# Strip sums on VectorE, expert weights loaded further ahead, a new order of products at the seams, and zero rows for dt

## The chip, the cores and the metric

The kernel runs on one core of one Trainium2 chip. The metric is the device time of one execution in microseconds, given as the median of three runs. Engines are named as in the profile: PE is TensorE (its matmuls; PEld its weight loads), DVE is VectorE, ACT is ScalarE, POOL is GpSimd, and SP is SyncE, which here only issues DMAs. ScalarE's queue issues DMAs too.

## The reference, cut to what matters

The input x has three images of 256 channels of 48 x 48 pixels. Four layers follow, each added to its input after a group norm of 32 groups:

```
x = x + layer0(gn(x))   # 1x1 convs, 2 blocks of attention + MLP, concat, 1x1 conv, norm, silu
x = x + layer1(gn(x))   # routing = sigmoid(mean(x) @ R); w = sum_e routing[e] * weight[e]; 3x3 conv
x = x + layer2(gn(x))   # 3x3 conv with one fixed weight and a bias
x = x + layer3(gn(x))   # Mamba block: in_proj, conv1d, selective scan, gate, out_proj
```

Layer 1 has eight experts, and each image has its own mixed 3x3 kernel of 256 x 256 channels. In layer 3, `dt = softplus(dt_raw @ dt_proj_w + dt_proj_b)` with a dt_raw of 16 columns, for 512 inner channels, and the state has 16 entries for each of them.

## The kernel before, in words

Channels lie on partitions: 256 channels are two tiles of 128 (`CT = 2`). An image of 2304 pixels is walked in six strips of 384 (`NCH = 6`, `CH = 384`). The images are taken in the order 2, 1, 0 (`ORDER`). Everything is float32.

Layer 0 ends, for each image, with an MLP stage and then a concatenation stage, six strips each. In `hidden` (L515 on) TensorE makes two products (L520) and ScalarE applies Gelu (L525, tile f); in `add_back` TensorE multiplies f (L531) and VectorE adds the result to `cur` (L535). In `concatenated` (L1031 on) TensorE runs eight matmuls a strip (L1035) over three loaded rows (`yc`) and `cur`; ScalarE applies Silu (L1040) into the resident image `xs[b]`; GpSimd adds the strip of the kernel's input `xc` (L1045), which is the residual. `yc` and `xc` are loaded by DMAs that stand in ScalarE's queue (L1021 and L1026). `take_stats` (L1047 on) then has VectorE take the statistics of a strip (L1049) for the next group norm; it is called one strip later.

Beside these stages runs the preparation of layer 1 for image 2. `mixed` is a generator: each step loads one piece of an expert's kernel (128 x 768, 384 KB, SP's queue, L251; eight experts times six pieces) and adds it with the expert's routing weight into `u`. The first expert's six pieces are copied and scaled on ScalarE (L294), the others are added on VectorE (L296). After 48 pieces, two steps of `kernel_transform` (L258 to L263, six operations each on VectorE) turn the three columns of the kernel into six: this is a Winograd form of the 3x3 convolution along one direction, in which 0 and 2 of the six stay the mixed columns themselves. `aside(n)` (above the loop at L1064 on) takes n steps of the mixing after each strip, and so sets the order by hand: two, or in image 0's hidden stage two and three in turn, and three in the concatenation stages; from the third strip of image 0 it takes all the rest. The pieces rotate through six buffers (`wst`). The order in which instructions are written is the order on each engine (`keep_order`).

At strip 3 of image 0 the pools for the first padded and transformed image are allocated and `input_transform` (L308 on) is called: ScalarE writes the normalised image with borders (`xpad`, L331), and VectorE makes the six transformed inputs `vt` of one half image in twelve operations (L345 to L356).

Layers 1 and 2 are six units (two layers by three images), each of two halves. `output` (L1641 on) makes, for a half h and an output tile m, six products of six matmuls each (`products`, L1634): products 1 and 3, then 4 and 5 (of each pair one is copied by ScalarE into `cb`, L1650, and VectorE makes their sum and difference), then 0 and 2; VectorE adds all of them into the image. Beside unit 0 the kernel of image 1 is mixed, beside unit 1 that of image 0. There, one of the six pieces of each expert is mixed on TensorE instead (L282).

In layer 3 the strips of all three images are walked as one chain, 18 strips, with VectorE's scan (L1949) as its heart. `project_dt` (L1323 on) multiplies dt_raw by the projection; its operand `k.dbc[: DTR + 1, :]` has 16 rows and a row of ones for the bias, out of a tile of 96 rows that also holds B and C of the scan. The weight tile `dtsb` has 17 rows, loaded from `dtw` (L1153), which the host code lays out. `take_sum` (L1362) multiplies the finished dt by u on VectorE; L1355 are the matmuls that it waits for, L1971 those of the output projection of the states.

Of the kernel before, what the change touches and what calls it, by code (L numbers as in the profile page):

```python
# [9 lines left out]
F32 = mybir.dt.float32  # L10
I32 = mybir.dt.int32
AF = mybir.ActivationFunctionType
ALU = mybir.AluOpType
# [71 lines left out]
def net(  # L85
# [160 lines left out]
        nc.vector.tensor_scalar(t[:, 1, :], sh, 1.0 / 6.0, None, ALU.mult)  # L246
        return t[:, 0, :], t[:, 1, :]

    def part_of_kernel(src, ct, dx):
        t = wst.tile([P, 3 * 256], F32, name="wconv")  # L250
        nc.sync.dma_start(t, src[ct * P : (ct + 1) * P, dx * 768 : (dx + 1) * 768])  # L251
        return t.rearrange("p (y o) -> p y o", y=3)

# [8 lines left out]
        nc.vector.tensor_tensor(u[:, 3, :, ct, :], t, g1, ALU.subtract)  # L262
        nc.vector.tensor_tensor(g1, t, g1, ALU.add)  # L263

    def mixed(b, pool, shared=False):

        u = weights[b] = pool.tile([P, 6, 3, CT, 256], F32, name="u")  # L270
        for e in range(EXPERTS):
            for ct in range(CT):
                for dx in range(3):
                    wt = part_of_kernel(we[e], ct, dx)
                    re = route[b][:, e : e + 1]
                    dst = u[:, dx, :, ct, :]
                    if shared and ct == CT - 1 and dx == 2:
                        flat = wt.rearrange("p y o -> p (y o)")
                        each = tmp.tile([P, P], F32, name="each")
                        nc.scalar.activation(each, ident, AF.Copy, scale=re)  # L280
                        for j in range(2):
                            nc.tensor.matmul(  # L282
                                bank[j], each, flat[:, j * 384 : (j + 1) * 384],
                                start=e == 0, stop=e == EXPERTS - 1,
                            )
                        if e == EXPERTS - 1:
                            for y, o, n in ((0, 0, 256), (1, 0, 128), (1, 128, 128), (2, 0, 256)):
                                at = y * 256 + o
                                j = at // 384
                                nc.scalar.copy(  # L290
                                    dst[:, y, o : o + n], bank[j][:, at - 384 * j : at - 384 * j + n]
                                )
                    elif e == 0:
                        nc.scalar.activation(dst, wt, AF.Copy, scale=re)  # L294
                    else:
                        nc.vector.scalar_tensor_tensor(dst, wt, re, dst, ALU.mult, ALU.add)  # L296
                    yield
        for ct in range(CT):
            kernel_transform(u, ct)
            yield  # L300
# [15 lines left out]
    def input_transform(b, h, sc, sh):  # L316

        rows = HR + 2
        size = rows * PW
        t = pad.tile([P, 4, CT * size + 2], F32, name="xpad")  # L320

        nc.gpsimd.memset(t[:, :, 0 : CT * size + 1 : PW], 0.0)  # L322
        at = (0 if h == 0 else HR + 1) * PW
        for ct in range(CT):
            nc.gpsimd.memset(t[:, :, ct * size + at : ct * size + at + PW], 0.0)
        lo = 1 if h == 0 else 0
        first = h * HR - 1 + lo
        for ct in range(CT):
            src = xs[b][:, ct, :].rearrange("p (j r c) -> p j r c", j=4, c=TW)
            dst = t[:, :, ct * size : (ct + 1) * size].rearrange("p j (r c) -> p j r c", c=PW)  # L330
            nc.scalar.activation(  # L331
                dst[:, :, lo : lo + HR + 1, 1:], src[:, :, first : first + HR + 1, :],
                AF.Identity, bias=sh[:, ct : ct + 1], scale=sc[:, ct : ct + 1],
            )

        def column(j, at):
            return t[:, j, at : at + CT * size].rearrange("p (r c) -> p r c", c=PW)[:, :, :TW]

        d = [column(j, at) for j, at in ((3, 0), (0, 1), (1, 1), (2, 1), (3, 1), (0, 2))]
        vt = vp.tile([P, 6, CT, (HR + 2) * TW], F32, name="vt")  # L340
        o = [vt[:, i].rearrange("p t (r c) -> p (t r) c", c=TW) for i in range(6)]
        c = pad.tile([P, CT * rows, TW], F32, name="wc")
        e = pad.tile([P, CT * rows, TW], F32, name="we")
        tt, stt = nc.vector.tensor_tensor, nc.vector.scalar_tensor_tensor
        stt(c, d[2], -4.0, d[4], ALU.mult, ALU.add)  # L345
        stt(e, d[1], -4.0, d[3], ALU.mult, ALU.add)
        tt(o[1], c, e, ALU.add)
        tt(o[3], c, e, ALU.subtract)
        tt(c, d[4], d[2], ALU.subtract)
        tt(e, d[3], d[1], ALU.subtract)  # L350
        stt(o[4], e, 2.0, c, ALU.mult, ALU.add)
        stt(o[5], e, -2.0, c, ALU.mult, ALU.add)
        tt(o[0], d[0], d[2], ALU.subtract)
        stt(o[0], o[0], 4.0, c, ALU.mult, ALU.add)
        tt(o[2], d[5], d[3], ALU.subtract)
        stt(o[2], e, -4.0, o[2], ALU.mult, ALU.add)  # L356
        return vt

    def routing(b, psum, tag, stats):
# [23 lines left out]
    with ExitStack() as l0:  # L383
# [627 lines left out]
        upools = {0: late_pool("up0")}  # L1011
        xpools[1] = late_pool("x1")
        xpools[0] = late_pool("x0", stack=last_pools)
        for b in ORDER:
            xs[b] = xpools[b].tile([P, CT, N], F32, name=f"x{b}")

# [7 lines left out]
        def tokens_of(b, c):  # L1024
# [3 lines left out]
            )  # L1028
            return xc

        def concatenated(b, c, yc, xc):  # L1031
            pz = pair()
            for m in range(2):
                for kt in range(4):
                    nc.tensor.matmul(  # L1035
                        pz[:, m, :CH], w("cv2", kt * 256 + m * P, P),
                        yc[:, kt, :] if kt < 3 else chunk(cur[b], c), start=kt == 0, stop=kt == 3,
                    )
            for m in range(2):
                nc.scalar.activation(  # L1040
                    chunk(xs[b][:, m, :], c), pz[:, m, :CH], AF.Silu,
                    bias=b2sh[:, m : m + 1], scale=b2sc[:, m : m + 1],
                )
            both = xs[b][:, :, c * CH : (c + 1) * CH]
            nc.gpsimd.tensor_tensor(both, both, xc, ALU.add)  # L1045

        def take_stats(b, c, stats):  # L1047
            for m in range(2):
                nc.vector.bn_stats(stats[m][:, c, :], chunk(xs[b][:, m, :], c))  # L1049

# [3 lines left out]
        ahead = [(rows_of(*chunks[z]), tokens_of(*chunks[z])) for z in range(3)]  # L1054
        rows_ahead, tokens_ahead = ([pair[j] for pair in ahead] for j in range(2))
        small_steps = [mlp_weights(i, 0)]
        mixing = mixed(2, upools[0])

        def aside(n):

# [9 lines left out]
        for n, b in enumerate(ORDER):  # L1070
            held = None
            for c in range(NCH):
                f = hidden(b, c)
                if held is not None:
                    add_back(i, *held)
                held = b, c, f
                aside(3 if n == 2 and c % 2 else 2)
            add_back(i, *held)
            stats = [
                small.tile([P, NCH, 6], F32, name=f"xst{m}", bufs=2) for m in range(CT)  # L1080
# [1 line left out]
            for c in range(NCH):  # L1082
                concatenated(b, c, rows_ahead.pop(0), tokens_ahead.pop(0))

                z = n * NCH + c + 2
                if 3 <= z < len(chunks):
                    tokens_ahead.append(tokens_of(*chunks[z]))
                if z + 1 < len(chunks):
                    rows_ahead.append(rows_of(*chunks[z + 1]))
                if c:  # L1090
                    take_stats(b, c - 1, stats)
                if b == 0 and c == 3:
                    vp = late_pool("vp", 2, last_pools)
                    pad = late_pool("pad", stack=last_pools)
                    first_v = input_transform(2, 0, *norms[2])
                aside(3 if n < 2 or c < 2 else 99)
            take_stats(b, NCH - 1, stats)
            if b:
                curpools[b].close()
# [34 lines left out]
    def w3_rooms():  # L1134
# [4 lines left out]
            block, ("w3sb", P, (NW3,)), ("winx", P, (CT, DI * P)), ("taps", P, (DI, DCONV, P)), ("convc", P, (DI * DCONV,)),  # L1139
            ("amat", P, (DI * DS,)), ("rep", P, (4, 32)), ("less", P, (2, P)), ("zero", P, (8,)),  # L1140
            ("xn0", P, (CT, XH)), ("xn1", P, (CT, XH)), ("xi", P, (3, XH)),
            ("dtsb", DTR + 1, (DI * P,)),
        ))
        rooms["xn"] = [w3v["xn0"], w3v["xn1"]]
        pieces = [wst.tile([P, 3 * 256], F32, name="wconv") for _ in range(6)]
# [177 lines left out]
    def project_dt(k, m0):  # L1323
        for j in range(2):
            m = m0 + j
            nc.tensor.matmul(
                bank[j], w3v["dtsb"][:, m * P : (m + 1) * P], k.dbc[: DTR + 1, :],
                start=True, stop=True,
            )

# [293 lines left out]
    with ExitStack() as l1:  # L1624
# [17 lines left out]
        def output(b, h, m, u, vt, bias):  # L1642

            xj = xs[b][:, m, :].rearrange("p (j n) -> p j n", j=4)[:, :, h * HN : (h + 1) * HN]
            tt, stt = nc.vector.tensor_tensor, nc.vector.scalar_tensor_tensor
            sums = []
            for i, j in ((1, 3), (4, 5)):
                pa, pb = products(u, vt, m, i), products(u, vt, m, j)
                cb = tmp.tile([P, HN], F32, name="cb")
                nc.scalar.copy(cb, pb)  # L1650
# [2 lines left out]
                sub = tmp.tile([P, HN], F32, name=f"sub{i}")  # L1653
                tt(sub, pa, cb, ALU.subtract)
                sums += [add, sub]
            p, q, r, s = sums
            for k, (minus, more, f) in enumerate(((p, r, 1.0), (q, s, 2.0), (p, r, 4.0), (q, s, 8.0))):
                if bias is None:
                    tt(xj[:, k], xj[:, k], minus, ALU.subtract)
                else:  # L1660
                    stt(xj[:, k], xj[:, k], bias[:, m : m + 1], minus, ALU.add, ALU.subtract)
                stt(xj[:, k], more, f, xj[:, k], ALU.mult, ALU.add)
            for i, k, f in ((0, 0, 1.5), (2, 3, 6.0)):
                stt(xj[:, k], products(u, vt, m, i), f, xj[:, k], ALU.mult, ALU.add)


        units = [(layer, b) for layer in range(2) for b in ORDER]
# [506 lines left out]
def _layout(i):  # L2174
# [39 lines left out]
        "w3": np.concatenate([w3[k] for k, _ in W3_WIDTHS], 1),  # L2214
        "w3x": l3["in_proj_w"][: DI * P].T,
        "convw": l3["conv_w"].reshape(DI, P, DCONV).transpose(1, 0, 2).reshape(P, -1),
        "dtw": np.concatenate([l3["dt_proj_w"].T, l3["dt_proj_b"][None]]),
    }


# [17 lines left out]
```

## Time and profile before

| | us |
|---|---|
| median of three runs | 3303.44 (3302.32 to 3303.94) |
| profiled execution | 3306.9 |
| its span, first to last instruction | 3305.1 |
| busy in it: PE, DVE, ACT, POOL | 3140.9, 2867.9, 2393.1, 1338.7 |
| mean granted TensorE clock | 0.983 of full |

The profile is one execution, taken on the slowest core, here the only one. It gives times of groups of instructions (a line of the kernel, an engine, an operation with its tiles), and names for idle time the event that ended it. A wait for several events is put down to the one that came last by the record. In rows of groups, "x42 | 44.8, 1119 | 0.0" is the number of instructions, their busy time in us, the mean of one in ns, and the idle time of the engine just before them. In rows of waits, the three numbers are the sum, the number of times, and the longest, in us. Layer 0's attention lasts until about 1322 us, the last MLP and concatenation stages until 1491, the convolutions until about 1997, and layer 3 to the end.

### The profile page before, as it was taken

The page shows a single profiled execution, that of the slowest core. Times are in us where ns is not written, and L with a number is a line of the kernel's source. Part 1 is how long each engine was busy: PE and PEld are TensorE (multiplying, and loading weights), DVE is VectorE, ACT ScalarE, POOL GpSimd, SP SyncE. Part 2 cuts the span into 40 slices and gives each one's busy share as a digit, 9 for nine tenths or more (in the row PEclk, how much of TensorE's full clock was granted, in tenths as well). Part 3 has the DMA queues.
Part 4 walks back from the last instruction along what each step waited for, and adds up shares of the span by engine and source line. Part 5 has one row for each costly group of instructions (what it writes and reads, how often), then busy time and mean ns, then how long its engine had stood idle before and what let it go on. Part 6 is the DMA issues. An engine that isn't in the chain of part 4 may idle for free.

```text
span 3305.1 us, 54212 instructions
## 1 busy us (share of the span) xinstructions
PE 3140.9 (95%) x20918; PEld 1557.1 (47%) x20918; DVE 2867.9 (87%) x3225; ACT 2393.1 (72%) x3675; POOL 1338.7 (41%) x457
## 2 busy tenths in 40 slices
PE   7999999999999999998999998999999999999996
PEld 4334343363343434556677774444444444444442
DVE  3799989967988999389985449999999999999998
ACT  2688888848888888332223458888888888888885
POOL 0000000000000000120000008999999999999998
PEclk9999999999999999999999999999999999999998
DMA  4000000010000000484621025555555555555552
GB/s 168 32 8 10 7 10 6 8 48 5 8 7 8 8 7 9 153 313 165 222 80 42 34 75 132 139 129 128 136 130 142 140 138 130 130 134 137 141 132 69
DMA packets 182657, 290.98 MB, mean 88 GB/s; under 512 B 34850, under 2 KB 148962, under 8 KB 180467
## 3 DMA queue, kind: packets, MB, share of 16 engines
q1 hardware_dynamic: 169426, 268.53, 30.1%
q10 hardware_dynamic: 12960, 18.88, 1.7%
q8 instruction: 166, 2.72, 0.3%
q14 instruction: 105, 0.85, 0.1%
HBM read 236.24 MB, written 50.64 MB: 87 GB/s over the span
## 4 chain that ended last, share of the span: by engine, by line
PE 55%; DVE 28%; ACT 8%; issue 5%; DMA 2%; POOL 1%; SPq 0%; DVEq 0%; ACTq 0%; POOLq 0%
DVE hs L1949 19%; PE ps_s L640 16%; PE acc L653 15%; PE ps_c L1634 8%; DVE hs L1896 3%; ACT ps_da L1941 2%; PE ps_s L1035 2%; PE ps_y L464 2%; DVE u L296 2%; PE ps_m L667 2%; PE ps_m L713 1%; PE acc L531 1%; PE ps_g L1229 1%; PE ps_s L520 1%; DMA wconv<-in_we 1%
## 5 line engine op out<-in xcount | busy, mean ns | idle before, releaser
L644 ACT ACTIVATE pt<-ps_s 128x1024 f32<-128x1024 f32 x972 | 942.4, 1022 | 154.7 <-PE ps_s L640 142.2
L1949 DVE TENSOR_TENSOR_SCAN hs<-ps_da,hs 128x385 f32<-128x385 f32 x1152 | 1002.6, 936 | 5.6 <-ACT ps_da L1941 4.5
L859 DVE TENSOR_TENSOR part<-part,pt 128x2048 f32<-128x2048 f32 x396 | 906.7, 2290 | 41.2 <-ACT pt L644 18.4
L1941 ACT ACTIVATE ps_da<-dtr,u 128x384 f32<-128x384 f32 x1136 | 642.0, 580 | 116.2 <-DVE hs L1949 105.5
L164 POOL TENSOR_TENSOR rstd<-ve,mhalf 128x2 f32<-128x2 f32 (+1 forms) x25 | 16.0, 642 | 1440.6 <-DVE ve L162 1440.6
L640 PE MATMUL ps_s<-q,kt 32*128 32x512 f32 (+1 forms) x4320 | 576.4, 592 | 0.1
L653 PE MATMUL acc<-pt,vt 128*32 128x512 f32 (+1 forms) x4320 | 520.9, 561 | 0.2
L1634 PE MATMUL ps_c<-vt,u 128*128 128x288 f32 x1728 | 431.9, 410 | 17.6 <-DVE u L263 9.0
L1957 POOL TENSOR_TENSOR hc<-hs,x 128x3072 f32<-128x3072 f32 x72 | 405.3, 5629 | 11.2 <-DVE hs L1949 6.7
L1957 POOL TENSOR_TENSOR hc<-hs,bc 128x3072 f32<-128x3072 f32 x71 | 400.2, 5636 | 9.8 <-POOL hs L1915 3.9
L1634 PEld LDWEIGHTS ps_c<-vt,u 128*128 128x128 f32 x1728 | 330.0, 192 | 114.3 <-DVE u L263 9.7
L640 PEld LDWEIGHTS ps_s<-q,kt 32*128 32x128 f32 x4320 | 195.2, 183 | 199.1 <-issue 120.2
L653 PEld LDWEIGHTS acc<-pt,vt 128*32 128x32 f32 x4320 | 94.4, 108 | 353.4 <-issue 326.7
L1971 PE MATMUL ps_y<-hc,u 128*32 128x384 f32 x2304 | 226.9, 514 | 2.9 <-POOL hc L1957 2.9
L1915 POOL TENSOR_TENSOR hs<-dtur,bc 128x1536 f32<-128x1536 f32 x72 | 209.8, 2913 | 0.0
L1280 PE MATMUL ps_g<-u 128*128 128x384 f32 x576 | 193.6, 488 | 11.6 <-ACT u L1276 11.6
L1915 POOL TENSOR_TENSOR hs<-dtur,x 128x1536 f32<-128x1536 f32 x70 | 203.5, 2907 | 0.0
L1280 PEld LDWEIGHTS ps_g<-u 128*128 128x128 f32 x576 | 107.5, 189 | 94.2 <-ACT u L1276 22.5
L1971 PEld LDWEIGHTS ps_y<-hc,u 128*32 128x32 f32 x2304 | 62.2, 112 | 144.0 <-issue 128.7
L1650 ACT COPY cb<-ps_c 128x288 f32<-128x288 f32 x48 | 19.2, 399 | 150.7 <-PE ps_c L1634 141.5
L322 POOL MEMSET xpad<- 128x212 f32 x12 | 5.7, 475 | 291.6 <-ACT xpad L1685 221.5
L1399 PE MATMUL ps_g<-u 128*128 128x384 f32 x288 | 106.6, 503 | 13.1 <-ACT sz L1407 7.7
(295 smaller groups left out, 4169.8 us busy)
## 6 DMA issues: line engine op xcount, KB each, us to landing
wconv<-in_we SPq DMA_DIRECT2D x144, 384.0 KB, 4.6
dtr<-dtd SPq DMA_DIRECT2D x284, 192.0 KB, 3.7
dtur<-dtud SPq DMA_DIRECT2D x284, 96.0 KB, 4.2
wconv<-xd SPq DMA_DIRECT2D x36, 384.0 KB, 4.0
x<-bcd SPq DMA_DIRECT2D x72, 192.0 KB, 4.9
dtd<-x SPq DMA_DIRECT2D x36, 384.0 KB, 3.0
bc<-bcd SPq DMA_DIRECT2D x72, 192.0 KB, 5.0
dtuq<-dtud SPq DMA_DIRECT2D x284, 48.0 KB, 2.0
```

What stands on the lines that cost most here:

```text
L640: nc.tensor.matmul(s[:, j, cols], kt[r, mt * P : (mt + 1) * P], q[r, :n], start=True, stop=True,)
L644: nc.scalar.activation(p[:, h0 : h0 + 2, :], s, AF.Exp)
L653: nc.tensor.matmul(acc[h * HD : (h + 1) * HD, :n], vt[:, mt, g * P + h * HD : g * P + (h + 1) * HD], p[:, h, cols], start=mt == 0, stop=mt ...
L859: ): nc.vector.tensor_tensor(part, first, p, ALU.add)
L1280: nc.tensor.matmul(bank[m % 2], w3v["taps"][:, m, tap, :], w3v["xi"][:, m % 3, tap : tap + CH], start=tap == 0, stop=tap == DCONV - 1,)
L1399: nc.tensor.matmul(bank[j], w("in", ct * 512 + m * P, P), k.xn[:, ct, DCONV - 1 :], start=ct == 0, stop=ct == CT - 1,)
L1634: nc.tensor.matmul(pc[:, :HN], u[:, i, dy, ct, m * P : (m + 1) * P], vt[:, i, ct, dy * TW : dy * TW + HN], start=ct == 0 and dy == 0, stop ...
L1915: nc.gpsimd.tensor_tensor(states(s)[:, :, 2:4, 1:], chunks[at].rows[m][1].unsqueeze(1).broadcast_to([P, 2, 2, CH]), b_rows(s, 0, 2), ALU.mult,
L1941: nc.scalar.activation(slots[n % 3][:, 1 : CH + 1], chunks[at].rows[m][0][:, q, :], AF.Exp, scale=amat[:, col : col + 1],)
L1949: nc.vector.tensor_tensor_scan(b, slots[(8 * s + part) % 3][:, : CH + 1], b, 0.0, ALU.mult, ALU.add)
L1957: nc.gpsimd.tensor_tensor(hc, tiles[s][:, :, :, 1:], cb.broadcast_to([P, 2, 4, CH]), ALU.mult)
L1971: nc.tensor.matmul(k.y_ps[32 * q : 32 * q + 32, :CH], fold, hc[:, g, q, :], start=False, stop=g == 1 and q in ends,)
```

## The change

In layer 0's last stages the strip sum goes from GpSimd in `concatenated` to VectorE in `take_stats`, directly ahead of the statistics and one strip later than before; so the buffer of `xc` is released by VectorE. `take_stats` is called ahead of the next loads. Pieces 6 to 13 of image 2's kernel get eight buffers of their own (`wst2`), on top of the six. Each hidden strip takes three steps of mixing. The rest of the mixing with the kernel transforms comes at strip 1 of image 0 instead of strip 2, and `input_transform` at strip 2 instead of 3, where the eight buffers are given back.

In layers 1 and 2, for the first half of a unit the transform writes its outputs in the order 0, 2, 4, 5, 1, 3 instead of 1, 3, 4, 5, 0, 2, and the first output tile takes its products in the order 0, 2, then 4 and 5, then 1 and 3. The second half and the other tile keep the old order.

In layer 3 the weights of `project_dt` get 79 rows of zeros, so that they have 96 rows, and the matmul runs over the whole tile `k.dbc`.

```diff
-    def part_of_kernel(src, ct, dx):
-        t = wst.tile([P, 3 * 256], F32, name="wconv")
+    def part_of_kernel(src, ct, dx, pool=None):
+        t = (pool or wst).tile([P, 3 * 256], F32, name="wconv")
...
-    def mixed(b, pool, shared=False):
+    def mixed(b, pool, shared=False, second=None):
...
-                    wt = part_of_kernel(we[e], ct, dx)
+                    at = (e * CT + ct) * 3 + dx
+                    wt = part_of_kernel(we[e], ct, dx, second if 6 <= at < 14 else None)
...
+        def odd():
+            stt(c, d[2], -4.0, d[4], ALU.mult, ALU.add)
+            stt(e, d[1], -4.0, d[3], ALU.mult, ALU.add)
+            tt(o[1], c, e, ALU.add)
+            tt(o[3], c, e, ALU.subtract)
+
+        def outer():
+            tt(o[0], d[0], d[2], ALU.subtract)
+            stt(o[0], o[0], 4.0, c, ALU.mult, ALU.add)
+            tt(o[2], d[5], d[3], ALU.subtract)
+            stt(o[2], e, -4.0, o[2], ALU.mult, ALU.add)
+
...
-        stt(c, d[2], -4.0, d[4], ALU.mult, ALU.add)
-        stt(e, d[1], -4.0, d[3], ALU.mult, ALU.add)
-        tt(o[1], c, e, ALU.add)
-        tt(o[3], c, e, ALU.subtract)
+        if h:
+            odd()
         tt(c, d[4], d[2], ALU.subtract)
         tt(e, d[3], d[1], ALU.subtract)
+        if not h:
+            outer()
         stt(o[4], e, 2.0, c, ALU.mult, ALU.add)
         stt(o[5], e, -2.0, c, ALU.mult, ALU.add)
-        tt(o[0], d[0], d[2], ALU.subtract)
-        stt(o[0], o[0], 4.0, c, ALU.mult, ALU.add)
-        tt(o[2], d[5], d[3], ALU.subtract)
-        stt(o[2], e, -4.0, o[2], ALU.mult, ALU.add)
+        if h:
+            outer()
+        else:
+            odd()
...
+        more_pools = ExitStack()
+        wst2 = late_pool("wst2", 8, more_pools)
...
+            added[b, c] = xc
+
+        def take_stats(b, c, stats):
             both = xs[b][:, :, c * CH : (c + 1) * CH]
-            nc.gpsimd.tensor_tensor(both, both, xc, ALU.add)
-
-        def take_stats(b, c, stats):
+            nc.vector.tensor_tensor(both, both, added.pop((b, c)), ALU.add)
...
-        mixing = mixed(2, upools[0])
+        mixing = mixed(2, upools[0], second=wst2)
...
-                aside(3 if n == 2 and c % 2 else 2)
+                aside(3)
...
+                if c:
+                    take_stats(b, c - 1, stats)
                 if 3 <= z < len(chunks):
                     tokens_ahead.append(tokens_of(*chunks[z]))
                 if z + 1 < len(chunks):
                     rows_ahead.append(rows_of(*chunks[z + 1]))
-                if c:
-                    take_stats(b, c - 1, stats)
-                if b == 0 and c == 3:
+                if b == 0 and c == 2:
+                    more_pools.close()
                     vp = late_pool("vp", 2, last_pools)
                     pad = late_pool("pad", stack=last_pools)
                     first_v = input_transform(2, 0, *norms[2])
-                aside(3 if n < 2 or c < 2 else 99)
+                aside(3 if n < 2 or c < 1 else 99)
...
-            ("dtsb", DTR + 1, (DI * P,)),
+            ("dtsb", 96, (DI * P,)),
...
-                bank[j], w3v["dtsb"][:, m * P : (m + 1) * P], k.dbc[: DTR + 1, :],
+                bank[j], w3v["dtsb"][:, m * P : (m + 1) * P], k.dbc,
...
+            def ends():
+                for i, k, f in ((0, 0, 1.5), (2, 3, 6.0)):
+                    stt(xj[:, k], products(u, vt, m, i), f, xj[:, k], ALU.mult, ALU.add)
+
+            first = h == 0 and m == 0
+            if first:
+                ends()
             sums = []
-            for i, j in ((1, 3), (4, 5)):
+            for i, j in ((4, 5), (1, 3)) if first else ((1, 3), (4, 5)):
...
-            p, q, r, s = sums
+            p, q, r, s = sums[2:] + sums[:2] if first else sums
...
-            for i, k, f in ((0, 0, 1.5), (2, 3, 6.0)):
-                stt(xj[:, k], products(u, vt, m, i), f, xj[:, k], ALU.mult, ALU.add)
+            if not first:
+                ends()
...
-        "dtw": np.concatenate([l3["dt_proj_w"].T, l3["dt_proj_b"][None]]),
+        "dtw": np.concatenate(
+            [l3["dt_proj_w"].T, l3["dt_proj_b"][None], np.zeros((95 - DTR, DI * P), np.float32)]
+        ),
```

More of the change, by code (lines that the diff above doesn't have):

```diff
@@ L1029, in tokens_of @@
             return xc
+        added = {}
         def concatenated(b, c, yc, xc):
```

## The prediction

> **What bounds the kernel now.** I read the rows of busy tenths first (which stage leaves which engine free), then the waits of TensorE over the one stage that the change touches, then its windows, and then the groups of VectorE and GpSimd there. Below, "pieces" are the 384 KB expert weights, "mixing" is L296 on VectorE (one step a piece), and times are microseconds of the profiled execution.
>
> ```profile
> PE   7999999999999999998999998999999999999996
> DVE  3799989967988999389985449999999999999998
> ```
>
> A slice is 82.6 us. Attention (to about 1322) and the scan of layer 3 (slices 24 on, from about 1997) hardly change; the scan is bound by VectorE, so time gained before it is kept whole. The change works between 1322 and 1700, slices 16 to 20.
>
> ```profile
> PE ps_c L1634 <- ACT u L294: 7.4, 1, 7.4
> PE acc L531 <- ACT f L525: 4.1, 1, 4.1
> PE ps_r L376 <- DVE pbc L373: 0.3, 1, 0.3
> ...
> PE ps_c L1634 <- DVE u L263: 7.2, 1, 7.2
> PE ps_g L282 <- DMA wconv<-in_we: 1.3, 2, 0.8
> ...
> PE ps_c L1634 <- DVE u L263: 1.8, 1, 1.8
> PE ps_c L1634 <- DVE u L262: 1.1, 1, 1.1
> ```
>
> The waits of TensorE over 1400 to 1500, 1500 to 1620 and 1620 to 1720: total, times, longest. There are four places: 4.1 before the last MLP's concatenation (at 1437.9 to 1441.9), 7.4 at the first convolution product ("seam A", 1490.7 to 1498.1), 7.2 between the first two images' convolutions ("seam B", 1584.2 to 1591.8), 1.8 and 1.1 at the next ("seam C", 1675.4). From 1700 to 2000 TensorE is busy 298.11 of 300: that stretch starts earlier by whatever the seams give.
>
> ```profile
> 1480.00:1500.00 20.00, 12.58 (x38) 7.45 (x37) 19.69 (x19) 10.50 (x13) 7.02 (x6) 0.89 0.46 157
> ...
> 1580.00:1600.00 20.00, 12.70 (x38) 8.38 (x37) 19.94 (x26) 12.76 (x18) 0.69 (x3) 0.74 0.67 230
> ```
>
> Windows: length, busy time of PE, PEld, DVE, ACT, POOL, granted clock, DMA share, GB/s. VectorE is full in both seams (19.69 and 19.94 of 20), TensorE is not. So the release that ends the 7.4 is named ACT, but the late engine is VectorE: the first product started at 1498.09, right after the transform L347 that it reads ended (1497.83). And the clock falls after each gap (0.89, 0.74): the first two products of unit 0 took 8.5 and of unit 1 9.1, against 6.14 (12 matmuls of 0.41 twice over, less overlap) later. A gap therefore costs 2 to 3 more than its length.
>
> ```profile
> L296 DVE SCALAR_TENSOR_TENSOR u<-wconv,route,u 128x768 f32<-128x768 f32 x42 | 44.8, 1119 | 0.0
> L1049 DVE BATCH_NORM_STATS2 xst<-x 128x6 f32<-128x384 f32 x30 | 15.3, 549 | 40.1 <-POOL x L1045 40.1
> ...
> L260 DVE SCALAR_TENSOR_TENSOR u<-u,wconv 128x768 f32<-128x768 f32 x2 | 3.5, 1755 | 0.0
> L262 DVE TENSOR_TENSOR u<-wconv,u 128x768 f32<-128x768 f32 x2 | 3.4, 1712 | 0.1
> ...
> L1045 POOL TENSOR_TENSOR x<-x,xc 128x768 f32<-128x768 f32 x18 | 36.9, 2052 | 93.8 <-ACT x L1040 78.7 <-DMA wconv<-in_we 15.2
> ```
>
> Groups between 1324 and 1498. The strip sum takes GpSimd 2052 ns, and whatever VectorE does beside it stretches: L260 1755 in the mean against 951 for its sister L258, which met no sum.
>
> **The change part by part.**
>
> *Strip sums to VectorE.* Added: 18 times a two-input 128x768 operation; the nearest row is L261, the same form, 958 ns: 18 x 0.96 = 17.3. Taken away: the stretching. Of the kernel transforms the eight instructions of L259, L260, L262 and L263 took 3.4 + 3.5 + 3.4 + 3.5 = 13.8 against 8 x 0.96 = 7.7: 6.2 back (unrounded). Of L296: 42 x (1.119 - 1.011, its median without sums) = 4.5 back. Net +6.6 over the stage, but VectorE idled 40.1 there, waiting for these same sums, so only the last strips count: in seam A four sums (strips 2 to 5) = +3.8 against -6.2. [...] by the row (2.45 instead of 0.96 beside a sum) it is 2.4 earlier. I take the row.
>
> *Eight more pieces, mixing a strip sooner.* No DMA more in number: the same 144 pieces, eight of them issued on SP's queue earlier, at a time when it is idle. Before the last concatenation 45 mixing steps are done instead of 39, so 6 x 0.95 = 5.7 of VectorE leave the way to seam A. ScalarE gets three first-expert pieces of 0.9 ahead of its activation f where it had two; TensorE's L531 there waits about 1.5 longer. The 4.1 wait goes in good part, for it was ScalarE held by its queue (a table load at 1440.0 that a piece let go, with the DMAs at 369 GB/s, share 1.02): -3.5. But in the last hidden stage six strips have 3 mixings instead of 2 or 3, 18 instead of 15, 2.9 more on VectorE ahead of pbc (L373), which TensorE's L376 waits for; I get +3.6 there in place of the 0.3 shown. Sum -3.5 + 3.6, about 0 (bounds -3.5 and +3.6): the last concatenation starts at 1459.2 as before and ends at 1490.7.
>
> *Order in seam A.* VectorE afterwards: sum 0 at 1467, twelve kernel transforms 1468.9 to 1480.1 (12 x 0.93), sum 1 at 1481, the input transform (12 of 0.8). ScalarE: the load of the next xc stands in its queue and now waits for VectorE's sum 1, then xpad (2.67) to 1484.7; input transform 1484.7 to 1494, its fourth output ready at 1489.4; then ScalarE's Silu of strip 3 (1.23), the second xpad to 1495.2 (it waits until the transform has read the first), Silu of strips 4 and 5 to 1498.3. The first product waits for those Silus' bank: 1498.5. What VectorE gains, ScalarE's queue gives back: +0.4. Bounds: with no hold the products could follow strip 5's Silu at 1492, -6; with every held step taken in full +3. I take the walk.
>
> *Unit 0.* VectorE still owes three sums, the statistics and the routing chain of the last image, among the first products: L186, L195 and L376 stand in TensorE's order there. I put +2.1 on the sixth product (bounds 0 and +4). Unit 0 ends at 1584.2 + 0.4 + 2.1 = 1586.7.
>
> *Seam B.* VectorE's mixing for the next image ends sooner by 6.2 + 5.7 - 3.8 = 8.1: at about 1575.5 for 1583.6. The new order puts products 0 and 2 first, which use mixed weights that no transform touches, so TensorE starts at once and has 6.1 of work until products 4 and 5, whose transform is then ready (about 1585). The wait of 7.6 (1584.2 to 1591.8) goes, with 2.5 of the slow clock after it.
>
> *Seam C.* The same order gives 6.1 of slack and VectorE is 8.1 ahead for a TensorE 7.6 ahead: of 1.8 + 1.1, I take 2.4 back (bounds 0 and 2.9).
>
> *Zero rows for dt.* L1326 contracts 96 rows instead of 17. Its duration should not move (481 at 17 rows; L1355 at 128 rows 486). Its weights' one load grows from 34 KB to 196 KB; it runs on SP's queue during layer 2's convolutions, where the DMA share is 0.16 and TensorE waits for nothing of it: 0. What can move is the clock: in the scan the clock is halved in six windows of 3.4 (at 2206.5, 2278.2 and so on), two in each image, and at six places VectorE waits for slow matmuls:
>
> ```profile
> DVE dtu L1362 <- PE ps_g L1355: 2.8, 3, 0.9
> DVE x L1362 <- PE ps_g L1355: 2.8, 3, 0.9
> ```
>
> Just ahead of each stand L1326's 17-row matmuls after 0.9 of idle (2192.5 to 2194.1); then L1971 takes 2.47 where it takes 1.5 elsewhere. [...] By the trace the window ahead of the dip was 75% busy (2.71 of 3.60 from 2191.0 to 2194.6)[...] and what sets it apart is the narrow matmuls in it; then the gain is up to 2.8 + 2.8 = 5.6. Loss has no cause that I can see. I lean to the trace: 4.0, as if four of the six dips went, since the 0.9 of idle ahead of L1326 remains.
>
> **Sum.** 0 + 0.4 + 2.1 - 7.6 - 2.5 - 2.4 - 4.0 = -14.0. The profiled execution took 3306.9 (span 3305.1 and 1.8 around it) and becomes 3292.9; the median before is 3303.4, 3.5 below that execution, and becomes 3289.4.
>
> **The rivals.**
>
> *The zero rows do nothing* (0.27): [...] against it, the dips' place. Seams alone: -10.0, 3293.4.
>
> *Seam A closes too* (0.10): if ScalarE isn't held by VectorE's sums, -6.4 more than forecast: 3283.
>
> *Moved, not gone* (0.14): VectorE stays the bound at 1500 to 1620 (19 of every 20), the new order only moves TensorE's wait from the first product to the third or fifth; of seams B and C 4 to 5 remain gained, no dt: about 3299.
>
> *Slower* (0.09): in the last two concatenations a strip gives VectorE a sum, two statistics and three mixings, 0.96 + 1.02 + 3 x 0.95 = 4.83, in a strip of 5.16 on TensorE. The sum stands in order behind mixings that wait for pieces; the next xc's load on ScalarE's queue waits for the sum, and the next Silu and yc stand behind that load. On GpSimd this ring was open. For it: GpSimd's sums waited 15.2 for DMA in this stage, and the queues moved 369 GB/s. Against it: eight pieces are already there. It binds from 0.33 of lateness a strip; over 12 strips it eats the 14.0 at 1.2 + 0.33 a strip, and at 2.2 the run is slower by 8: 3312.
>
> **How the numbers follow.** Forecast (0.40): 3289.4, itself 3284 to 3294. A measurement can tell about 0.2% (6.6) from no change, so faster is below 3296.8. Faster: 0.40 + 0.10 + 0.23 of the 0.27 = 0.73; same: 0.14 + 0.04 = 0.18; slower 0.09. The range reaches down to 3279 (closed seam A with dt in full) and up to 3302 (most of "moved"), and leaves out the slower case and the ends.
>
> **What would show it.** Right: no sum on GpSimd, L259 to L263 at 0.95; no TensorE wait of 7 at seam B and the clock at 1.0 there; still about 7 at seam A, with ScalarE's xc issue waiting for VectorE; six half-clock windows of the scan gone and with them the waits of L1362. Wrong: new waits of L1653 for VectorE inside unit 0 or 1, concatenation strips longer than 5.2 with ScalarE held at an xc load, or a first product later than 1501.

## The result, and the profile after

The changed kernel takes 3290.59 us (median of 7 runs, 3288.46 to 3291.73) and the kernel before, in the same series, 3303.94 (7 runs, 3299.53 to 3304.06): 13.3 us less, a ratio of 0.9961 with a 95% interval of 0.9952 to 0.9971. The forecast was 3289.4, 14.0 less.

The profiled execution took 3288.56 (span 3286.8), 2.0 below its median, and that of before lay 3.0 above its own; so the pair of profiles differs by 18.3, of which 5 come from the choice of executions. Its times, on the axis of the span, with those of before:

| moment | before | after | shift |
|---|---|---|---|
| first matmul of image 2's concatenation | 1352.0 | 1349.9 | -2.2 |
| start of image 0's concatenation | 1459.2 | 1456.7 | -2.5 |
| its end | 1490.7 | 1492.2 | +1.6 |
| first product of unit 0 | 1498.1 | 1495.7 | -2.4 |
| unit 0, last tile, first copy into cb | 1569.7 | 1566.4 | -3.3 |
| unit 1, second tile, first copy into cb | 1621.0 | 1608.2 | -12.8 |
| end of layer 2's last product | 1995.3 | 1981.7 | -13.6 |
| end of the span | 3305.1 | 3286.8 | -18.3 |

(The two copies stand at the same place of both orders.) The first -2.2 lies ahead of anything that the change touches in this stage. The gain comes in one step, between units 0 and 1, and in the scan. The waits of TensorE over the same three stretches (engine, line, what it waited for: total, times, longest):

```profile
PE ps_c L1653 <- ACT x L1057: 3.4, 1, 3.4
PE ps_r L389 <- DVE pbc L386: 2.9, 1, 2.9
PE ps_s L1052 <- DMA yc<-ycat: 2.8, 1, 2.8
PE acc L544 <- ACT f L538: 2.7, 2, 1.9
...
PE ps_g L283 <- DMA wconv<-in_we: 1.4, 1, 1.4
PE ps_gm L186 <- DVE mv L183: 1.3, 1, 1.3
...
PE ps_g L283 <- DMA wconv<-in_we: 1.7, 1, 1.7
PE ps_c L1653 <- DVE x L1667: 0.6, 1, 0.6
```

Up to the first product the change gives nothing: 3.4 + 2.9 + 2.8 + 2.7 = 11.8, and before it was 7.4 + 4.1 + 0.3 = 11.8. In place of one wait of 7.4 and one of 4.1 there are four of about 3. The waits for the kernel transform, 7.2 and 1.8 + 1.1, are gone. The windows around the two seams:

```profile
1480.00:1500.00 20.00, 13.82 (x37) 8.23 (x36) 17.12 (x25) 9.00 (x11) 0.69 (x3) 0.83 0.25 80
...
1580.00:1600.00 20.00, 20.00 (x82) 15.28 (x81) 17.55 (x26) 16.14 (x22) 1.39 (x6) 1.00 0.53 177
```

In the second row TensorE is busy 20.00 of 20 at clock 1.00, where it had 12.70 at 0.74. In the first it is hardly better than before (13.82 for 12.58), though VectorE now has 2.9 to spare: something else holds the seam. The groups of VectorE from 1322 to 1496 show that it isn't stretched any more:

```profile
L297 DVE SCALAR_TENSOR_TENSOR u<-wconv,route,u 128x768 f32<-128x768 f32 x42 | 40.0, 1007 | 0.0
...
L1065 DVE TENSOR_TENSOR x<-x,xc 128x768 f32<-128x768 f32 x16 | 15.3, 956 | 27.6 <-ACT x L1057 27.6
...
L260 DVE SCALAR_TENSOR_TENSOR u<-u,wconv 128x768 f32<-128x768 f32 x2 | 1.9, 952 | 0.0
```

L297 takes 1007 ns in the mean for 1119 before (busy time by number, which leaves overlaps out, 40.0 / 42 = 0.95 for 44.8 / 42 = 1.07), L260 took 0.95 for 1.76, and a sum costs 0.956, as estimated. (Before, not every instruction beside a sum was longer: by the record L258 of 1476.92 took 0.95 within GpSimd's sum of 1476.19 to 1479.54.) What holds the seam is in the timeline (start, length, engine or its queue, line):

```profile
1477.96 0.95 DVE L1065 TENSOR_TENSOR x<-x,xc 128x768 f32<-128x768 f32 x1
...
1478.94 0.37 ACTq L1041 DMA_DIRECT2D xc<-in_x  x1
...
1479.36 0.53 ACTq L1036 DMA_DIRECT2D yc<-ycat  x1
...
1479.93 2.67 ACT L332 ACTIVATE xpad<-x,six 128x1200 f32<-128x1200 f32 x2 [6.36 <-issue]
...
1485.40 3.61 PE L1052 MATMUL ps_s<-yc,w0b 128*128 128x384 f32 x6 [2.77 <-DMA yc<-ycat]
...
1490.47 2.67 ACT L332 ACTIVATE xpad<-x,six 128x1200 f32<-128x1200 f32 x2 [6.75 <-DVE we L345]
```

VectorE's sum of strip 1 stands behind twelve kernel transforms. It ends at 1478.91, and the next xc load, which reuses the buffer that it frees, goes out at 1478.94. Until then this load stands at the head of ScalarE's queue, and yc, the padding and the Silus stand behind: ScalarE idles 6.36 (put down to "issue" in the row, since what held it was a load), yc goes out at 1479.36, some 6 us after ScalarE had become free (1473.6), and TensorE, finding no yc, waits 2.77 and then runs six matmul instructions at a mean granted clock of 0.60 (3.61 for 2.10). The concatenation takes 35.6 for 31.5. Later the second padding waits 6.75 for VectorE's transform, with two Silus behind it that release the first product.

In the scan, the waits of VectorE from 2040 on:

```profile
DVE hs L1975 <- ACT ps_da L1967: 4.3, 16, 0.3
DVE hs L1922 <- ACT wconv L1443: 3.6, 17, 0.2
DVE wconv L1443 <- PE ps_g L1433: 1.7, 1, 1.7
DVE sz L2026 <- PE ps_y L1997: 0.9, 1, 0.9
```

The two rows for L1362, 2.8 each, have no successor. (The prediction placed the half-clock windows at 2206.5 and 2278.2. These were times of the record's own axis, which begins 11.3 before the span; in the profile's times they are 2195.2 and 2266.9, right at the slow L1971 of 2194.83. The 3.41 ahead of the first are then 2191.8 to 2195.2, where TensorE is busy 2.69 of 3.41, and not the 2191.0 to 2194.6 of the prediction's 75%.)

### The profile page after: what moved, and what is told of

The parts are those of the page before. It is cut to its first block, busy times and chain, and to the rows that moved or that the text cites. A ratio compares the mean times of both kernels' runs of the same rounds, so it can differ in the third digit from the quotient of the medians.

```text
span 3286.8 us, 54171 instructions
## 1 busy us (share of the span) xinstructions
PE 3121.7 (95%) x20918; PEld 1552.2 (47%) x20918; DVE 2873.8 (87%) x3243; ACT 2391.8 (73%) x3675; POOL 1301.8 (40%) x439
## 4 chain that ended last, share of the span: by engine, by line
PE 56%; DVE 28%; ACT 8%; issue 4%; DMA 2%; POOL 1%; SPq 0%; ACTq 0%; DVEq 0%; POOLq 0%
DVE hs L1975 19%; PE ps_s L653 16%; PE acc L666 15%; PE ps_c L1653 9%; DVE hs L1922 3%; ACT ps_da L1967 3%; PE ps_s L1052 2%; PE ps_y L477 2%; PE ps_m L680 2%; PE ps_g L1248 2%; PE ps_m L726 1%; PE acc L544 1%; POOL hc L1983 1%; PE ps_s L533 1%; PE ps_g L1255 1%
## 5 line engine op out<-in xcount | busy, mean ns | idle before, releaser
L164 POOL TENSOR_TENSOR rstd<-ve,mhalf 128x2 f32<-128x2 f32 (+1 forms) x25 | 15.9, 639 | 1525.1 <-DVE ve L162 1469.9
L1418 PE MATMUL ps_g<-u 128*128 128x384 f32 x288 | 107.9, 508 | 13.6 <-ACT sz L1426 8.1
```

Source lines behind the costliest of these rows:

```text
L1418: nc.tensor.matmul(bank[j], w("in", ct * 512 + m * P, P), k.xn[:, ct, DCONV - 1 :], start=ct == 0, stop=ct == CT - 1,)
```

## The experiments

Eleven further kernels ran in three series. "Difference" is the median against the median of before in the same series; "stage" is the time from image 2's first concatenation matmul to the end of layer 2's last product, in the one profiled execution; "dips" are the stretches at half clock (0.50) in the profile's record of the granted clock between 2100 and 3190, inside the scan.

| kernel | median | difference | ratio, 95% interval | stage | dips |
|---|---|---|---|---|---|
| before | 3303.94 | | | 643.3 | 6 |
| changed | 3290.59 | -13.3 | 0.9961 (0.9952 to 0.9971) | 631.8 | 0 |
| dt alone | 3299.93 | -3.9 | 0.9987 (0.9978 to 0.9995) | 637.6 | 0 |
| seams alone | 3294.02 | -9.8 | 0.9970 (0.9959 to 0.9980) | 634.3 | 4 |
| order alone | 3295.15 | -8.6 | 0.9972 (0.9961 to 0.9983) | 632.7 | 6 |
| sums alone | 3301.39 | -2.4 | 0.9994 (0.9988 to 1.0001) | 642.3 | 4 |
| changed, xc on GpSimd's queue | 3286.57 | -16.4 | 0.9948 (0.9934 to 0.9962) | 624.7 | 0 |
| order + dt | 3288.22 | -14.7 | 0.9950 (0.9937 to 0.9964) | 631.5 | 0 |
| order + dt + sums | 3285.77 | -17.2 | 0.9946 (0.9932 to 0.9959) | 625.7 | 0 |
| the same, xc on GpSimd's queue | 3287.74 | -16.2 | 0.9948 (0.9935 to 0.9962) | 629.3 | 0 |
| changed, sums on GpSimd | 3292.21 | -11.7 | 0.9965 (0.9953 to 0.9977) | 635.4 | 0 |
| 32 rows for dt | one run, 3301.7 | | | 639.6 | 4 |
| 64 rows for dt | one run, 3301.9 | | | 640.7 | 0 |

Four of them (before, dt alone, 32 and 64 rows) have the same code in the stage and lie between 637.6 and 643.3: a single stage length tells no difference under some 5 us. The intervals of the medians reach 2 to 5 us to each side of a difference from before. The single runs with 32 and 64 rows serve for their traces alone; their times lie within the spread of before (3297 to 3310).

**dt alone.**

```diff
-            ("dtsb", DTR + 1, (DI * P,)),
+            ("dtsb", 96, (DI * P,)),
...
-                bank[j], w3v["dtsb"][:, m * P : (m + 1) * P], k.dbc[: DTR + 1, :],
+                bank[j], w3v["dtsb"][:, m * P : (m + 1) * P], k.dbc,
...
-        "dtw": np.concatenate([l3["dt_proj_w"].T, l3["dt_proj_b"][None]]),
+        "dtw": np.concatenate(
+            [l3["dt_proj_w"].T, l3["dt_proj_b"][None], np.zeros((95 - DTR, DI * P), np.float32)]
+        ),
```

> The kernel before with the 96-row dt matmul alone. Theory [...]: the six half-clock windows of the scan and the six waits of L1362 for L1355 (2.8 + 2.8 in the profile before) go, and the time falls by 4 to 6 us. Rival [...]: about six dips again, and within 1 us of before.

Measured: -3.9, no dip inside the scan, and no wait of L1362. What the theory expected came, at the lower end of its 4 to 6.

**Seams alone**: the changed kernel with these lines put back, so against the changed kernel

```diff
-                bank[j], w3v["dtsb"][:, m * P : (m + 1) * P], k.dbc,
+                bank[j], w3v["dtsb"][:, m * P : (m + 1) * P], k.dbc[: DTR + 1, :],
```

> The changed kernel with the 17-row dt matmul back. Theory: the parts add up, so it keeps what the seams bring, 8 to 11 us faster than before, and the six dips of the scan and the waits of L1362 are there again. Rival [...]: the dips are fewer than six although the matmul has 17 rows, and the time is that of the changed kernel, 13 us faster than before.

Measured: -9.8, with four dips and waits of L1381 (L1362 before) for L1374 of 1.9 + 1.9. -3.9 and -9.8 add up to -13.7 for the 13.3 of the whole, so the parts add as far as these intervals tell. On the dips the rival is right in part: they are four and not six with the same 17 rows. But none of the five profiles with 17 or 32 rows is without them.

**32 and 64 rows**, to see with how many rows the dips go; the weights get as many rows. The edit with 32 (the other has 64 in its place):

```diff
-                bank[j], w3v["dtsb"][:, m * P : (m + 1) * P], k.dbc[: DTR + 1, :],
+                bank[j], w3v["dtsb"][:, m * P : (m + 1) * P], k.dbc[:32, :],
```

> The kernel before with 32 rows (15 of them zero) in the dt matmul instead of 17. Theory A [...]: 32 rows look like 17, and four to six half-clock windows in the scan remain, with waits of L1362 for L1355. Theory B [...]: fewer dips, two or less.

> The kernel before with 64 rows (47 of them zero) in the dt matmul. Theory [...]: no half-clock window inside the scan and no wait of L1362 for L1355. Rival [...]: four to six windows as with 17 and 32 rows.

The waits of VectorE in the scan with 32 rows:

```profile
DVE dtu L1362 <- PE ps_g L1355: 1.9, 2, 0.9
DVE x L1362 <- PE ps_g L1355: 1.9, 2, 0.9
```

With 64 rows these rows are missing. The windows from 2100 to 3200, of 32 rows and then of 64 rows (busy PE, PEld, DVE, ACT, POOL, clock, DMA share, GB/s):

```profile
2100.00:3200.00 1100.00, 1036.47 (x4917) 519.34 (x4916) 1088.74 (x1298) 966.10 (x1919) 1082.67 (x308) 0.99 0.56 135
```

```profile
2100.00:3200.00 1100.00, 1034.41 (x4928) 520.05 (x4927) 1091.79 (x1301) 968.64 (x1925) 1086.54 (x309) 1.00 0.56 136
```

The clock is 0.99 with 32 rows and 1.00 with 64, and VectorE, the bound, does 3 us more work in the same time. All kernels with 17 or 32 rows (five profiles) have four to six dips, all with 64 or 96 (eight profiles) none. VectorE's waits for the slow matmuls (L1362 for L1355 before) go the same way: 6 before and with the order alone, 5 with the sums alone, 4 in seams alone and with 32 rows, none in the eight. So theory A came with 32 rows and the theory with 64.

The profile of before tells a little more. Each of its six dips lasts 3.41. Here are two stretches of that length, each with the one after it:

```profile
2191.79:2195.20 3.41, 2.69 (x13) 1.13 (x17) 3.41 (x5) 2.76 (x8) 3.41 (x2) 1.00 0.68 199
2195.20:2198.61 3.41, 3.41 (x18) 1.21 (x11) 3.41 (x5) 3.21 (x6) 3.41 (x1) 0.50 0.67 175
...
2406.83:2410.24 3.41, 1.93 (x7) 0.86 (x7) 3.41 (x7) 3.00 (x7) 3.41 (x2) 1.00 1.07 202
2410.24:2413.65 3.41, 3.41 (x22) 1.22 (x22) 3.41 (x4) 2.85 (x7) 3.41 (x2) 1.00 0.64 206
```

TensorE works longer in the first (2.69 against 1.93), and yet the clock is at 0.50 after that one and at 1.00 after the other. In the first 1.55 of the time are L1326 with its 17 rows, in the other 0.15. That is one pair: what sets the clock the runs do not show.

Nor do they part the rows of zeros from the real data that the longer operand brings with it. Of the 64 rows of `k.dbc`, 33 hold data (dt_raw, the ones and B); the rest are zeros themselves. Measured is only that no dip is left with 64 rows, of whose weights 47 are zeros.

**Order alone**: the edits of `input_transform` and `output`, nothing else.

```diff
+            first = h == 0 and m == 0
+            if first:
+                ends()
...
-            for i, j in ((1, 3), (4, 5)):
+            for i, j in ((4, 5), (1, 3)) if first else ((1, 3), (4, 5)):
```

> The kernel before with only the new order of the transform and of the products in the first half and tile of each unit; sums on GpSimd, six buffers, old mixing pace. Theory (the new order needs VectorE to be ahead as well): the seam between units 0 and 1 shrinks by up to the 6.1 us of two products, the wait reappears in part at the third product; -5 to -8 us. Rival (VectorE's lateness is only moved by two products, and it is the bound from 1500 to 1620): under 2 us. Second rival (the order alone is the whole gain of the seams): -8 to -11.

The waits of TensorE over the three stretches:

```profile
PE ps_c L1646 <- DVE vt L350: 8.2, 1, 8.2
PE acc L543 <- ACT f L537: 2.9, 1, 2.9
PE ps_r L388 <- DVE pbc L385: 1.1, 2, 0.7
...
PE ps_g L282 <- DMA wconv<-in_we: 2.4, 1, 2.4
...
PE ps_g L282 <- DMA wconv<-in_we: 1.9, 2, 1.2
PE ps_c L1646 <- ACT cb L1669: 0.4, 1, 0.4
```

-8.6, nearly the whole of the seams, by the second rival; the interval (5.6 to 12.9) also holds the theory's 5 to 8, so the trace has to decide. The first product still waits 8.2 with GpSimd's sums in the way, and yet nothing is left of the 7.2 of seam B: two products, 6.1, are enough for the transform that was late, without VectorE being ahead, and no wait reappears at the third. My theory, that the order needs the rest of the change, falls.

**Sums alone.**

```diff
-            nc.gpsimd.tensor_tensor(both, both, xc, ALU.add)
+            nc.vector.tensor_tensor(both, both, added.pop((b, c)), ALU.add)
```

> The kernel before with only the strip sums on VectorE ahead of the statistics, and the statistics ahead of the next loads; old order, buffers and pace. Theory: the kernel transforms L259 to L263 take 0.95 us again and end some 2.4 earlier, but ScalarE's queue is held at each xc load until VectorE's sum, so between -4 and +2 us. Rival (the ring of sum, xc load and Silu binds in the concatenation stages without the pieces ahead): slower by 3 to 10 us, with ScalarE held at its xc loads.

Its waits from 1400 to 1500, then the larger ones from 1500 to 1620:

```profile
PE ps_c L1637 <- DVE vt L347: 4.5, 1, 4.5
PE acc L531 <- ACT f L525: 2.0, 1, 2.0
PE ps_r L376 <- DVE pbc L373: 0.6, 2, 0.4
...
PE ps_c L1637 <- DVE u L263: 6.5, 1, 6.5
PE ps_g L282 <- DMA wconv<-in_we: 5.1, 3, 3.2
```

Up to the first product 7.1 for 11.8; then TensorE waits 5.1 for pieces (1.3 before) and 6.5 for the transform. What was gained ahead of unit 0 is lost at its end. The -2.4 lies in the theory's range, and its interval reaches no change. With the old order this is the exchange of waits that I feared for the whole change.

**The order and dt, without and with the sums**, no pieces ahead and the old pace. The second of them against the changed kernel:

```diff
-                    wt = part_of_kernel(we[e], ct, dx, second if 6 <= at < 14 else None)
+                    wt = part_of_kernel(we[e], ct, dx)
...
-                aside(3)
+                aside(3 if n == 2 and c % 2 else 2)
...
-                if b == 0 and c == 2:
-                    more_pools.close()
+                if b == 0 and c == 3:
...
-                aside(3 if n < 2 or c < 1 else 99)
+                aside(3 if n < 2 or c < 2 else 99)
```

> The new order of products and the 96-row dt matmul, with the sums on GpSimd, six buffers and the old mixing pace. Theory (the order is all of the seams' gain, and sums, buffers and pace cancel against the yc wait and the held ScalarE): within 1.5 us of the changed kernel, 12 to 14 us faster than before. Rival (VectorE has to be ahead): 3 to 6 us slower than the changed kernel.

> The changed kernel without the eight pieces ahead, the three steps a strip and the strip sooner: new order, 96-row dt, sums on VectorE. Theory (the sums alone brought the first product some 6 us forward from the start of the first concatenation, and lost it at the seam between units 0 and 1, which the new order closes): 2 to 5 us faster than the changed kernel. Rival (units 0 and 1 are then bound by the loads of the pieces, as the 5.1 us of L282 waiting for them with the sums alone suggest): the same as the changed kernel within 1.5 us.

-14.7 and -17.2. Order and dt alone do what the changed kernel does (-13.3), so its other parts together bring nothing that these medians show. With the sums, and the order to keep what they give, the waits up to the first product are about as short as with the sums alone:

```profile
PE ps_c L1649 <- DVE vt L350: 5.1, 1, 5.1
PE ps_r L388 <- DVE pbc L385: 1.4, 2, 0.9
PE acc L543 <- ACT f L537: 1.0, 1, 1.0
```

7.5 in all, and no yc wait: the sum that stands behind the twelve transforms is then that of strip 2 (1484.3), when the last yc has long been sent for (1471.7). In the changed kernel the transforms come a strip sooner and the last yc is caught behind them. This kernel has the lowest median of all, 3.9 below the changed one as its theory had it, but the two intervals overlap (0.9932 to 0.9959, 0.9952 to 0.9971).

**Sums back on GpSimd in the changed kernel**, the fourth field of the table by sums and by pieces ahead with the pace.

```diff
-            added[b, c] = xc
...
+            nc.gpsimd.tensor_tensor(both, both, xc, ALU.add)
...
-            nc.vector.tensor_tensor(both, both, added.pop((b, c)), ALU.add)
```

> The changed kernel with only the strip sums back on GpSimd, in the concatenation: new order, 96-row dt, pieces ahead and quicker pace stay. It fills the fourth field of a table of two by two (sums; pieces ahead with the pace). Theory (the pieces ahead with the pace cost some 4 us wherever the sums are, because VectorE reaches pbc late and f waits for the third first-expert piece): slower than order and dt alone by 1 to 4 us, that is 11 to 14 faster than before. Rival (they hurt only together with the sums, by the held xc loads): the same as or better than order and dt alone, 15 us or more faster than before.

| difference from before | six buffers, old pace | pieces ahead, new pace |
|---|---|---|
| sums on GpSimd | -14.7 | -11.7 |
| sums on VectorE | -17.2 | -13.3 |

Pieces and pace cost 3.0 in the upper row and 3.9 in the lower; the sums give 2.5 and 1.6. Both signs come out twice, as the theory had it, but each pair of intervals overlaps: the sizes stay open. Of the theory's two reasons the trace of this run shows one: against order and dt alone TensorE waits 4.4 for 2.9 for f, but 0.9 for 1.1 for pbc. In the three profiles with both pieces ahead and sums on VectorE TensorE waits 2.4 to 3.4 for pbc, in the ten others 0.3 to 2.2.

**xc on GpSimd's queue**, in the changed kernel and in the one with order, dt and sums.

```diff
-            nc.scalar.dma_start(
+            nc.gpsimd.dma_start(
                 xc, x[b, :, c * CH : (c + 1) * CH].rearrange("(t p) n -> p t n", p=P)
             )
```

> The changed kernel with the loads of xc issued on GpSimd's queue instead of ScalarE's. Theory (ScalarE, held by xc loads that wait for VectorE's sums, gives back what VectorE gains): ScalarE no longer idles 6.4 ahead of the first xpad, the yc load goes out at once so that the 2.8 wait of the concatenation for yc goes, the concatenation of image 0 takes 31 to 32 us again, and the first product starts 3 to 5 us earlier; -2 to -5 us against the changed kernel if the later seams let it through. Rival (VectorE's own order sets the first product, and the stages after it are bound by the pieces' loads): the yc wait goes, the time moves by under 1.5 us, the wait reappearing inside unit 0.

> New order, 96-row dt and sums on VectorE without the pieces ahead and the quicker pace, and with the xc loads on GpSimd's queue. Theory (held ScalarE still costs: there it waited 8.0 for VectorE's sum 1 ahead of the first xpad, and VectorE then 2.2 for that xpad): the xpad is done early, VectorE goes on without that 2.2, and the first product starts about 2 us earlier than in the run without the pieces ahead; 1 to 3 us faster than that run, 18 to 20 faster than before. Rival (the later seams and the pieces' loads bound it): the same within 1.5 us.

In the changed kernel (-16.4 for -13.3, with intervals that overlap, so that the trace has to show the cause) the first stretch shows

```profile
PE ps_r L389 <- DVE pbc L386: 3.4, 2, 3.0
PE ps_c L1653 <- ACT x L1057: 3.3, 1, 3.3
PE acc L544 <- ACT f L538: 1.6, 2, 1.2
```

The yc wait is gone, the concatenation takes 31.1 for 35.6, and its start lies 34.4 ahead of the first product for 39.0 (39.0 too in "seams alone", whose code there is the same): the held queue was the cause, at 4.6 us of path. The first padding goes out at 1477.7 with no idle time before it. What remains, 3.3, is the second padding's wait for VectorE with Silus behind. In the other kernel the seam shrank too (3.7 for 5.1), but TensorE then waited 2.7 for pieces in unit 0 in place of 0.8, and the time didn't fall (-16.2 for -17.2): there the rival holds. The three fastest kernels, all with the sums on VectorE, lie at 16 to 17 below before, and their intervals do not part them.

## Why the prediction was right, step by step

*The total* was right: 14.0 forecast, 13.3 measured, and the two terms that I put highest, the order at seam B and the rows of zeros, are the ones that brought it. That the sum came within 0.7 is luck in part: the interval is 9.6 to 15.9, and a term that came out 3.0 better (unit 0) stands against one that came out 1.6 worse (seam C).

*Stage before seam A*: 0 forecast, -0.4 measured (-2.5 less the -2.2 before the stage). The 4.1 for f became 2.7, and pbc went from 0.3 to 2.9, where I had 3.9. The 3.5 that I had put on the eight pieces was taken from one profile: f waits 2.7 to 4.1 in the four profiles with the code of before there, and 1.6 to 4.4 in the four with the pieces ahead, so the pieces gain nothing at f that the profiles show.

*Seam A*: +0.4 forecast; from the start of the concatenation to the first product 39.0 for 38.9. The number is right, the way to it only half. That VectorE was the late engine before, although the row names ACT, holds: with the same code, dt alone has `PE ps_c L1634 <- DVE vt L347: 6.2, 1, 6.2`. And ScalarE did hold the padding and the Silus. But I had the concatenation end at 1490.7, with a gap of 7.8; it ended at 1492.2 with a gap of 3.4, since the same held queue also delayed yc. That was the ring of my slower rival, and it closed at one strip, where twelve transforms stand ahead of the sum, and not at each of twelve strips: elsewhere VectorE had 27.6 of idle time ahead of the sums.

*Unit 0*: +2.1 forecast, -0.9 measured to the last tile. The wait for the statistics came (L186, 1.3). But two waits for pieces, 1.3 in sum, did not come there, and the gap ahead of unit 0 was shorter by 4.0, so that less of it ran at the low clock (0.84 granted over its first 9.0, for 0.77) and TensorE was busy 69.40 for 70.28: I had charged the new wait and credited neither.

*Seam B*: -10.1 forecast, -9.5 measured (from -3.3 to -12.8). Right in size, wrong in one reason: VectorE's lead, 8.1 forecast and 6.1 measured (its last transform for unit 1 starts at 1588.69 for 1594.83), wasn't needed, as the order alone shows. The forecast rival "moved, not gone" rested on the same belief that VectorE at 19 of 20 bounds units 0 and 1. It doesn't: with TensorE busy 194.81 of 200 from 1500 to 1700 (188.44 before), VectorE kept up at 190.25. A busy share of 95% was no proof of a bound while one late item explained each wait.

*Seam C*: -2.4 forecast, -0.8 measured. The transforms' waits went (2.9 to none), and waits for pieces, 1.7 in that stretch, and one of 0.6 for VectorE came. I had set nothing in their place.

*Zero rows*: -4.0 forecast, -3.9 by median, -4.7 in the pair of profiles. The rival that they do nothing is out: four to six dips with 17 and 32 rows, none with 64 and 96. The trace that I leaned to was right as to the place of the dips; that the narrow matmuls cause them was my estimate, which the runs bear out for the number of rows alone. My discount for the 0.9 of idle was wrong: all dips went, though TensorE waits for x ahead of these matmuls as before (14.2 from 2100 to 3200, for 13.4). The waits they caused sum to 5.6, the medians show 3.9 with an interval of 1.7 to 7.3, which holds both.

*Sums off GpSimd*: taking them off gave 2.5, 1.6 and 2.4 in three comparisons, and none alone is clear of noise. The row that I took (2.45 instead of 0.96 beside a sum) pointed the right way as far as the sign shows; the worth of the sums was nowhere near the 36.9 us that GpSimd was relieved of.

## What to carry to other kernels

If one engine is late at a seam, first look for work of the waiting engine whose operands are ready without the late step, and put it ahead: here two such products, 6.1 us of work, were enough, and that reordering alone was worth 8.6 of the 9.8 us that all parts of the change gained at the seams. When an operation moves to another engine, look at which queue its released buffer reopens: here one xc load that waited for VectorE held what stood behind it in ScalarE's queue, and ScalarE idled 6.36 us. And look at matmuls of few rows when the granted clock dips in the middle of busy work: 79 rows of zeros in the weights cost 5 ns a matmul here (486 for 481), and with them the six dips in the scan became none.

## What the runs showed of the hardware that was not expected

In the profile of before, 3.41 us in which TensorE was busy 2.69, 1.55 of it with 17-row matmuls, were followed by half clock (0.50); 3.41 us in which it was busy 1.93, 0.15 of it with those, were followed by full clock (1.00). 17 and 32 rows gave four to six half-clock stretches in the scan, 64 and 96 rows none, though the added weights are zeros and the matmuls last as long (481 ns at 17 rows, 486 at 96, the medians). And in the thirteen profiles, whose kernels have the same attention code, the first concatenation starts between 1347.6 and 1355.1: 7.5 us, over half the gain. So short stages are to be compared from a moment inside the run, not from its start.
